# A four-layer graph network kernel: a short last piece of columns summed inside the piece in front of it, its lists placed between the next layer's prologue steps, and x loaded once

## The chip, the cores and the metric

The kernel runs on one NeuronCore of a Trainium2 chip. Five engines work side by side, each through its own instruction stream in order: TensorE (matrix products and transposes, called PE in the profile, with its weight loads as PEld), VectorE (DVE), ScalarE (ACT), GpSimd (POOL) and SyncE (SP), which issues nearly all DMAs here. The metric is the device time of one execution in microseconds; the time quoted is the median of three runs.

## The reference

Inputs are x, 2708 rows of 128 numbers, and adj, a sparse 2708 x 2708 matrix (about 0.6% of the off-diagonal entries are not zero, and the diagonal is full). Four layers follow one another; each normalises x, applies relu and adds its result to x.

```python
# layer 0
h = relu(layernorm(x))
x = x + (adj.T @ h) * (1 / adj.sum(axis=0))[:, None]      # infinite factors count as 0
# layer 1
h = relu(layernorm(x))
messages = gelu(s[:, None, :] + d[None, :, :] + msg_b)    # s, d: two products of h
aggregated = einsum('ijd,ij->id', messages, adj)
x = x + layernorm(gelu([h, aggregated] @ upd_w.T + upd_b) + h) * ln_w + ln_b
# layer 2: adj @ h and a GRU cell; layer 3: masked attention over adj, two heads
```

## The kernel before

**Tiling.** N = 2708 is cut into 22 row tiles of 128 (the last has 20 rows). GROUPS (line 48) puts them together in fours: six groups, five of 512 rows and a last one of 148. Layer 0 walks over pieces of columns c, one for each group, and inside a piece over the six row groups s. An item (c, s) is one block of adj, about 512 rows by 512 columns. LAST = 5 is the short piece, whose columns are the last 148 outputs and some 80 columns more for the lists.

**What an item does.** load_cut (line 299) brings the block of adj from HBM into one of RING = 4 buffers named a; the short piece's blocks z0 to z5 have buffers of their own. mask_near (line 317) copies, on GpSimd, the blocks of 124 columns that cross the diagonal and clears the diagonal in them, from the pool "marked" (6 buffers). list_cut (line 337) finds for each row and each block of 124 columns the eight greatest entries and their places on VectorE (max and max_index); layer 1 works from these lists. work_cut (line 353) transposes the block on TensorE, four 128 x 128 transposes into one of two PSUM banks p_T, copies it on ScalarE into one of seven buffers aT and lets SP write it to adjT in HBM for layers 2 and 3 (lines 382 to 387). Between the transposes stand the products of layer 0: adj.T @ h0, where h0 carries a column of ones that gives the degrees (line 368); the sums stay in PSUM over all six items of a piece, in the pool sump (line 287): two buffers of two banks. Then ScalarE counts entries by their sign (line 398), and on the diagonal items c = s it takes the diagonal out of a product that GpSimd made in the tile dg (lines 411 and 412, four buffers).

**What a finished piece needs.** invert (line 416) takes the reciprocal of the degrees, spread (line 435) scales the sums on ScalarE and adds them to x on GpSimd; sum_rows, sum_squares and normal_rows (lines 249 to 271) normalise the new rows on ScalarE and GpSimd, turn_rows (line 214) transposes them, destinations and split_destinations (lines 223 and 240) make the vectors d of layer 1 as three bf16 parts. enter and rows (lines 443 and 455) are the same steps on VectorE for pieces 4 and 5.

**The order.** All of this stands under manual_schedule: the order of the statements is the order on every engine, written out by hand. The loop over items (lines 473 to 529) is, for each item: mask_near, the lists, work_cut, load_cut of the item three ahead, then one step for an earlier piece. While piece 0 runs, ScalarE computes the row statistics of x that give h0. After the loop stand enter(4), the six items of the short piece without their lists, with turn_rows and destinations of piece 3 among them, and the masks of the short piece. The prologue of layer 1 (lines 993 to 1005) then names its steps one by one: list_last(s) makes the short piece's lists of one row group, rank, select_rows, describe, finish_rows, fetch_both and place prepare a row tile, pass_on and columns send its column numbers through HBM. After it come the periods of layer 1, one for each row tile, and layers 2 and 3.

**x.** Lines 78 and 79 clear the last tile of x and load its first four tiles; lines 460 and 461 do the same once more under the manual schedule, ahead of the first adj block. load_rest (line 80) brings the other tiles in six DMAs.

Of the kernel before, what the change touches and what calls it, by code (L numbers as in the profile page):

```python
# [30 lines left out]
P = 128  # L31
# [29 lines left out]
def listed_layers(ctx: ExitStack, tc: tile.TileContext, x, adj, w, out, flag):  # L61
# [18 lines left out]
    def load_rest():  # L80
        for t, k in GROUPS[1:-1]:
            nc.sync.dma_start(xs[:, t : t + k, :], x[t * P : (t + k) * P, :].rearrange("(t p) d -> p t d", p=P))
        nc.sync.dma_start(xs[:, FULL - 1, :], x[(FULL - 1) * P : FULL * P, :])
        nc.sync.dma_start(xs[0:TAIL, FULL, :], x[FULL * P : N, :])
# [98 lines left out]
    some4 = keep.tile([P, 4, NB, S], BF16, name="some4")  # L183
# [101 lines left out]
    marked = l0.enter_context(tc.tile_pool(name="l0n", bufs=6))  # L285
    turned = l0.enter_context(tc.tile_pool(name="l0t", bufs=7))
    sump = l0.enter_context(tc.tile_pool(name="l0p", bufs=2, space=PSUM))
# [65 lines left out]
    def work_cut(c, s):  # L353
# [6 lines left out]
        if s == 0:  # L360
            accs[c] = sump.tile([P, 2 * CH], F32, name="sums")
        pv = accs[c].rearrange("p (b x) -> p b x", b=2)[:, :, 0 : 2 * (D + 1)].rearrange("p b (q d) -> p b q d", q=2)

        def products(n):
            m = size(n)
            for q in range(tk):
                k, e = size(t0 + q), (t0 + q) * P - lo
                nc.tensor.matmul(  # L368
                    pv[0:k, q // 2, q % 2, :], a[0:m, n - g0, e : e + k], h0[0:m, n, :],
# [36 lines left out]
        if c == s:  # L406
            for q in range(gk):
                m = size(g0 + q)
                e = (g0 + q) * P - lo
                dg = marked.tile([P, P], F32, name="dg", bufs=4)  # L410
# [5 lines left out]
    def invert(g):  # L416
# [3 lines left out]
        if k == 4:  # L420
            sums = accs[g].rearrange("p (b x) -> p b x", b=2)[:, :, 0 : 2 * (D + 1)]
            sums = sums.rearrange("p b (q d) -> p b q d", q=2)[:, :, :, D]
            nc.vector.reciprocal(r.rearrange("p (b q) -> p b q", b=2), sums)
        else:
            nc.vector.reciprocal(r, last_sums[:, 0:k, D])
# [3 lines left out]
    def sums_of(g, q):  # L429

        if g == LAST:
            return last_sums[:, q, 0:D]
        return accs[g][:, q // 2 * CH + q % 2 * (D + 1) : q // 2 * CH + q % 2 * (D + 1) + D]
# [26 lines left out]
    nc.vector.memset(xs[:, NT - 1, :], 0.0)  # L460
    nc.sync.dma_start(xs[:, 0:4, :], x[0 : 4 * P, :].rearrange("(t p) d -> p t d", p=P))
# [11 lines left out]
    order = [(c, s) for c in range(LAST) for s in range(len(GROUPS))]  # L473
    for i, (c, s) in enumerate(order):
        g0, gk = GROUPS[s]
        mask_near(c, s)
# [7 lines left out]
        work_cut(c, s)  # L484
        if i > 0 and i - 1 + RING < len(order):
            load_cut(*order[i - 1 + RING])
        if c == LAST - 1:
            load_cut(LAST, s)

        if c == 0:  # L490
            for stage, g in (
                ((sum_rows, 1), (sum_rows, 2), (sum_squares, 1), (sum_rows, 3), (sum_squares, 2), (normal_rows, 1)),
# [7 lines left out]
        elif s == 0:  # L500
            invert(c - 1)
        elif s == 2:
            spread(c - 1)
        elif s == 3:
            sum_rows(*GROUPS[c - 1])
        elif s == 4:
            sum_squares(*GROUPS[c - 1])
        elif s == 5:
            normal_rows(h, *GROUPS[c - 1])
        if c > 1 and s == 0:  # L510
            turn_rows(c - 2)
        if c > 1 and s == 1:
            destinations(c - 2)
        if c > 1 and s == 3:
            split_destinations(c - 2)

# [15 lines left out]
    for s in range(len(GROUPS)):  # L532
        work_cut(LAST, s)
        if s == 1:
            turn_rows(LAST - 2)
        if s == 3:
            destinations(LAST - 2)
    for q, k in ((0, P), (1, TAIL)):
        nc.scalar.copy(last_sums[0:k, q, :], accs[LAST][0:k, q * (D + 1) : (q + 1) * (D + 1)])
# [27 lines left out]
    with (  # L567
# [411 lines left out]
        def list_last(s):  # L979
            g0, gk = GROUPS[s]  # L980
            for n in range(g0, g0 + gk):
                list_cut(LAST, s, n)

        def count_first(_):
            nc.vector.tensor_scalar(some4, val[:, 0:4, :, :], 0.0, None, ALU.is_gt)
            with nc.allow_low_precision("counts up to 8"):
                nc.vector.reduce_sum(rows_n[:, 0:4, :], some4, AX.X)
# [890 lines left out]
```

## Time and profile before

| | us |
|---|---|
| median of three runs | 1073.86 |
| the three runs | 1072.23, 1073.86, 1077.45 |
| the profiled execution | 1074.57 |
| its span, first to last instruction | 1072.8 |
| layer 0 and layer 1's prologue | 0 to 288 |
| layer 1's periods | 288 to about 590 |
| layers 2 and 3 | about 590 to the end |

The span in four stretches, with the busy time of each engine, the number of its instructions in brackets, then the TensorE clock that was granted (1.00 is full speed), the share of time that the 16 DMA engines were busy, and GB/s:

```profile
0.00:288.00 288.00, 212.64 (x1633) 190.45 (x1634) 226.75 (x1381) 194.29 (x505) 85.39 (x234) 0.88 0.70 235
288.00:590.00 302.00, 285.65 (x4089) 280.29 (x4087) 233.50 (x563) 193.06 (x593) 246.80 (x246) 0.98 0.33 104
590.00:790.00 200.00, 183.29 (x818) 103.13 (x816) 111.07 (x324) 69.00 (x186) 82.26 (x60) 0.96 0.48 159
790.00:1072.80 282.80, 248.77 (x2104) 240.07 (x2102) 222.53 (x476) 60.28 (x143) 57.69 (x59) 0.96 0.04 11
```

A line of a time-ordered view reads: start, duration, engine, line of the program, operation, output and input, shape, how many were merged into the line; in square brackets how long the engine stood idle before it and what released it.

### The profile page before, as it was taken

The page shows a single profiled execution, that of the slowest core. Times are in us where ns is not written, and L with a number is a line of the kernel's source. Part 1 is how long each engine was busy: PE and PEld are TensorE (multiplying, and loading weights), DVE is VectorE, ACT ScalarE, POOL GpSimd, SP SyncE. Part 2 cuts the span into 40 slices and gives each one's busy share as a digit, 9 for nine tenths or more (in the row PEclk, how much of TensorE's full clock was granted, in tenths as well). Part 3 has the DMA queues.
Part 4 walks back from the last instruction along what each step waited for, and adds up shares of the span by engine and source line. Part 5 has one row for each costly group of instructions (what it writes and reads, how often), then busy time and mean ns, then how long its engine had stood idle before and what let it go on. Part 6 is the DMA issues. An engine that isn't in the chain of part 4 may idle for free. (4 is left out here: it accounts for less than half of the span.)

```text
span 1072.8 us, 23407 instructions
## 1 busy us (share of the span) xinstructions
PE 930.4 (87%) x8632; PEld 813.9 (76%) x8632; DVE 793.9 (74%) x2742; ACT 516.6 (48%) x1427; POOL 472.1 (44%) x596
## 2 busy tenths in 40 slices
PE   3798887893599999999979968999979999999982
PEld 3798887862599999999879934444478899989981
DVE  7689979738877788878768164656678987997783
ACT  5978867763366567666736522433322200330142
POOL 5322312322598778897858263444320200250042
PEclk9899998985699999999989988999999999999996
DMA  8599898922143333332132046566410000000000
GB/s 258 193 341 317 272 362 269 322 78 80 55 125 124 116 105 123 115 99 93 57 109 83 29 168 214 187 221 227 123 38 21 7 9 1 2 15 6 2 16 15
DMA packets 77667, 133.91 MB, mean 125 GB/s; under 512 B 14044, under 2 KB 30032, under 8 KB 77542
## 3 DMA queue, kind: packets, MB, share of 16 engines
q1 hardware_dynamic: 75726, 129.52, 36.6%
q10 hardware_dynamic: 1816, 2.80, 0.9%
q8 instruction: 70, 1.15, 0.5%
q14 instruction: 55, 0.45, 0.1%
HBM read 85.67 MB, written 30.87 MB: 109 GB/s over the span
## 5 line engine op out<-in xcount | busy, mean ns | idle before, releaser
L725 POOL TENSOR_SCALAR put<-count,line,value 128x128 f32<-128x128 f32 x176 | 197.4, 1135 | 44.3 <-DVE value L714 31.2
L1124 PE MATMUL att<-hv,wt 128*128 128x129 f32 x1672 | 193.4, 276 | 9.0 <-DVE wt L1094 9.0
L1124 PEld LDWEIGHTS att<-hv,wt 128*128 128x128 f32 x1672 | 189.8, 192 | 11.9 <-DVE wt L1094 8.9
L807 PE MATMUL p_m<-s,sel 128*128 128x128 bf16 x1452 | 163.5, 222 | 8.0 <-ACT g L819 7.9
L811 PE MATMUL p_m<-d,cols 124*128 124x128 bf16 (+1 forms) x1452 | 164.2, 222 | 7.0 <-DVE cols L756 6.9
L1094 DVE SCALAR_TENSOR_TENSOR wt<-row,lift,mask 128x1024 f32<-128x1024 f32 (+1 forms) x132 | 138.7, 1082 | 23.2 <-PE att L1124 23.2
L121 POOL TENSOR_TENSOR n_r<-n_r,minus_half 128x4 f32<-128x4 f32 (+1 forms) x27 | 39.1, 1447 | 241.0 <-DVE n_r L120 237.3
L832 PE MATMUL agg<-put,g 128*128 128x128 f32 (+1 forms) x968 | 122.9, 279 | 0.0
L1263 PE MATMUL p_agg<-a,hs 128*128 128x512 f32 (+2 forms) x264 | 111.0, 563 | 12.5 <-DMA a<-adjT 12.5
L368 PE MATMUL sums<-h,a 128*128 128x129 f32 (+1 forms) x880 | 119.6, 284 | 0.0
L807 PEld LDWEIGHTS <-sel 128*128 128x128 bf16 x1452 | 105.0, 99 | 11.5 <-issue 10.9
L832 PEld LDWEIGHTS agg<-put,g 128*128 128x128 f32 x968 | 113.6, 192 | 0.0
L382 PE MATMUL p_T<-ident,a 128*128 128x128 f32 (+1 forms) x440 | 73.9, 291 | 44.1 <-ACT aT L386 32.8
L368 PEld LDWEIGHTS sums<-h,a 128*128 128x128 f32 (+1 forms) x880 | 111.3, 200 | 0.8
L811 PEld LDWEIGHTS <-cols 124*128 124x128 bf16 (+1 forms) x1452 | 104.2, 99 | 7.3 <-DVE cols L756 7.3
L734 ACT ACTIVATE put<-mine,value 128x128 f32<-128x128 bf16 x308 | 100.5, 391 | 0.0
L819 ACT ACTIVATE g<-p_m 128x512 f32<-128x512 f32 x132 | 72.6, 551 | 55.9 <-PE agg L832 43.5
L1263 PEld LDWEIGHTS p_agg<-a,hs 128*128 128x128 f32 (+1 forms) x264 | 48.2, 196 | 61.9 <-issue 53.5
L382 PEld LDWEIGHTS p_T<-ident,a 128*128 128x128 f32 (+1 forms) x440 | 54.6, 148 | 52.5 <-ACT aT L386 36.4
L349 DVE MAX8 val<-a 128x8 f32<-128x124 f32 x342 | 79.4, 274 | 19.0 <-DMA a<-in_adj 19.0
L351 DVE FIND_INDEX8 col<-val,a 128x8 uint16<-128x124 f32 x342 | 92.3, 283 | 0.0
L386 ACT COPY aT<-p_T 128x512 f32<-128x512 f32 (+2 forms) x122 | 66.1, 565 | 42.8 <-PE p_T L382 35.0
(284 smaller groups left out, 1560.1 us busy)
## 6 DMA issues: line engine op xcount, KB each, us to landing
adjT<-aT SPq DMA_DIRECT2D x105, 256.0 KB
a<-adjT SPq DMA_DIRECT2D x20, 1280.0 KB
spread<-passed SPq DMA_DIRECT2D x22, 704.0 KB
later<-sel SPq DMA_DIRECT2D x22, 616.0 KB
a<-in_adj SPq DMA_DIRECT2D x5, 1152.0 KB
a<-in_adj SPq DMA_DIRECT2D x5, 1120.0 KB
a<-in_adj SPq DMA_DIRECT2D x5, 1088.0 KB
a<-in_adj SPq DMA_DIRECT2D x5, 1056.0 KB
```

What stands on the lines that cost most here:

```text
L349: nc.vector.max(val[0:m, n, b, :], v)
L351: nc.vector.max_index(col[0:m, n, b, :], val[0:m, n, b, :], v)
L368: nc.tensor.matmul(pv[0:k, q // 2, q % 2, :], a[0:m, n - g0, e : e + k], h0[0:m, n, :], start=(n == 0 and q % 2 == 0), stop=(n == NT - 1), ...
L382: nc.tensor.transpose(p[0:k, i * iw + q * P : i * iw + q * P + m], a[0:m, q, e : e + k], ident[0:m, 0:m])
L725: nc.gpsimd.tensor_scalar(st["put", 0][:, b, :], count, st["line"][:, b : b + 1], st["value"][:, b : b + 1], ALU.is_equal, ALU.mult,)
L734: nc.scalar.activation(st["put", 1][:, b - HP, :], st["mine"][:, b - HP, :], AF.Identity, scale=st["value"][:, b : b + 1])
L807: nc.tensor.matmul(p[:, b - b0, :], st["sel"][:, b, :], s3[:, q, t % 2, :], start=(q == 0), stop=False)
L811: nc.tensor.matmul(p[:, b - b0, :], st["cols"][0:kb, b, :], d3[0:kb, b, q, :], start=False, stop=(q == 2))
L832: nc.tensor.matmul(agg, g[:, b - 4 * k, :], put, start=(b == 0), stop=False)
L1094: nc.vector.scalar_tensor_tensor(wt[:, 0:n], row[:, k, c : c + n], lift[:, j, k : k + 1], mask[:, j, c : c + n], op0=ALU.max, op1=ALU.mult,)
L1124: nc.tensor.matmul(banks[s // 3][:, s % 3, :], wt[:, q * P : (q + 1) * P], hv[:, j, k, :], start=(v < 2 and s // 3 not in touched), stop=( ...
L1263: nc.tensor.matmul(pa[:, 0:n], h[0:k, j, :], a[0:k, j - j0, 0:n], start=(j == 0), stop=(j == NT - 1))
```

## The change

x is loaded once: the second clearing and load are gone, and load_rest has three DMAs. The sums of a piece lie in one-bank tiles, four buffers of one bank instead of two of two, so that the short piece takes one. In the loop, mask_near is called one item ahead; load_cut and the invert of the piece before stand in front of work_cut; the short piece's blocks are loaded in piece 3 instead of piece 4; the steps for an earlier piece move one item forward or so; and from item (4,1) on each item of piece 4 is followed by work_cut of the short piece for the row group in front. Only the last row group of the short piece is left after the loop. Lists of the short piece are made row by row between the prologue's steps: row 0 before the first rank, rows 1 to 3 and their count behind it, the others later. The buffers of "marked" go from 6 to 8, those of dg from 4 to 2.

```diff
--- before.py
+++ after.py
@@ -78,9 +78,8 @@
     nc.vector.memset(xs[:, NT - 1, :], 0.0)
     nc.sync.dma_start(xs[:, 0:4, :], x[0 : 4 * P, :].rearrange("(t p) d -> p t d", p=P))
     def load_rest():
-        for t, k in GROUPS[1:-1]:
+        for t, k in ((4, 8), (12, FULL - 12)):
             nc.sync.dma_start(xs[:, t : t + k, :], x[t * P : (t + k) * P, :].rearrange("(t p) d -> p t d", p=P))
-        nc.sync.dma_start(xs[:, FULL - 1, :], x[(FULL - 1) * P : FULL * P, :])
         nc.sync.dma_start(xs[0:TAIL, FULL, :], x[FULL * P : N, :])
 
     ident = const.tile([P, P], F32, name="ident")
@@ -180,7 +179,7 @@
     ends4 = keep.tile([P, NB, R], BF16, name="ends4")
     rows_n = keep.tile([P, NT, NB], BF16, name="rows_n")
     ends = keep.tile([P, NT, NB], BF16, name="ends")
-    some4 = keep.tile([P, 4, NB, S], BF16, name="some4")
+    some4 = keep.tile([P, 3, NB, S], BF16, name="some4")
     later = keep.tile([P, NB, E], BF16, name="later")
     nc.gpsimd.memset(later, 0.0)
     xb = [keep.tile([P, NB, C], BF16, name=f"xb{q}") for q in range(2)]
@@ -282,9 +281,9 @@
     rows_a = l0.enter_context(tc.tile_pool(name="l0", bufs=RING))
     once0 = l0.enter_context(tc.tile_pool(name="l0h", bufs=1))
     pool = l0.enter_context(tc.tile_pool(name="l0k", bufs=2))
-    marked = l0.enter_context(tc.tile_pool(name="l0n", bufs=6))
+    marked = l0.enter_context(tc.tile_pool(name="l0n", bufs=8))
     turned = l0.enter_context(tc.tile_pool(name="l0t", bufs=7))
-    sump = l0.enter_context(tc.tile_pool(name="l0p", bufs=2, space=PSUM))
+    sump = l0.enter_context(tc.tile_pool(name="l0p", bufs=4, space=PSUM))
     turnp = l0.enter_context(tc.tile_pool(name="l0q", bufs=2, space=PSUM))
     h0 = once0.tile([P, NT, D + 1], F32, name="h0")
     offdiag = once0.tile([P, P], F32, name="offdiag")
@@ -358,15 +357,17 @@
         lo = window(c)[0]
         a = cuts[c, s]
         if s == 0:
-            accs[c] = sump.tile([P, 2 * CH], F32, name="sums")
-        pv = accs[c].rearrange("p (b x) -> p b x", b=2)[:, :, 0 : 2 * (D + 1)].rearrange("p b (q d) -> p b q d", q=2)
+            accs[c] = [
+                sump.tile([P, CH], F32, name="sums")[:, 0 : 2 * (D + 1)].rearrange("p (q d) -> p q d", q=2)
+                for _ in range(0, tk, 2)
+            ]
 
         def products(n):
             m = size(n)
             for q in range(tk):
                 k, e = size(t0 + q), (t0 + q) * P - lo
                 nc.tensor.matmul(
-                    pv[0:k, q // 2, q % 2, :], a[0:m, n - g0, e : e + k], h0[0:m, n, :],
+                    accs[c][q // 2][0:k, q % 2, :], a[0:m, n - g0, e : e + k], h0[0:m, n, :],
                     start=(n == 0 and q % 2 == 0), stop=(n == NT - 1), skip_group_check=True,
                 )
 
@@ -407,7 +408,7 @@
             for q in range(gk):
                 m = size(g0 + q)
                 e = (g0 + q) * P - lo
-                dg = marked.tile([P, P], F32, name="dg", bufs=4)
+                dg = marked.tile([P, P], F32, name="dg", bufs=2)
                 nc.gpsimd.tensor_tensor(dg[0:m, 0:m], a[0:m, q, e : e + m], ident[0:m, 0:m], ALU.mult)
                 nc.scalar.activation(
                     dg[0:m, 0:m], dg[0:m, 0:m], AF.Copy, accum_out=own[0:m, g0 + q : g0 + q + 1]
@@ -417,20 +418,15 @@
 
         t, k = GROUPS[g]
         r = inv[:, t : t + k]
-        if k == 4:
-            sums = accs[g].rearrange("p (b x) -> p b x", b=2)[:, :, 0 : 2 * (D + 1)]
-            sums = sums.rearrange("p b (q d) -> p b q d", q=2)[:, :, :, D]
-            nc.vector.reciprocal(r.rearrange("p (b q) -> p b q", b=2), sums)
-        else:
-            nc.vector.reciprocal(r, last_sums[:, 0:k, D])
+        for b in range(0, k, 2):
+            sums = last_sums if g == LAST else accs[g][b // 2]
+            nc.vector.reciprocal(r[:, b : b + 2], sums[:, :, D])
         nc.vector.tensor_scalar(lim[:, 0:k], r, FMAX, None, ALU.min)
         nc.vector.scalar_tensor_tensor(r, r, FMAX, lim[:, 0:k], op0=ALU.is_le, op1=ALU.mult)
 
     def sums_of(g, q):
 
-        if g == LAST:
-            return last_sums[:, q, 0:D]
-        return accs[g][:, q // 2 * CH + q % 2 * (D + 1) : q // 2 * CH + q % 2 * (D + 1) + D]
+        return (last_sums if g == LAST else accs[g][q // 2])[:, q % 2, 0:D]
 
     def spread(g):
 
@@ -457,8 +453,6 @@
         scale_rows(tiles_of(h, t, k), tiles_of(xs, t, k), *factors(*state.pop(("m", g))), AF.Relu)
 
     ordered.enter_context(tc.manual_schedule())
-    nc.vector.memset(xs[:, NT - 1, :], 0.0)
-    nc.sync.dma_start(xs[:, 0:4, :], x[0 : 4 * P, :].rearrange("(t p) d -> p t d", p=P))
     load_cut(0, 0)
     load_rest()
     for s in range(1, RING):
@@ -471,9 +465,9 @@
         nc.gpsimd.memset(wheres[q], 0.0)
 
     order = [(c, s) for c in range(LAST) for s in range(len(GROUPS))]
+    mask_near(0, 0)
     for i, (c, s) in enumerate(order):
         g0, gk = GROUPS[s]
-        mask_near(c, s)
         list_cut(c, s, g0)
         if i == 0:
             scale_rows(
@@ -481,15 +475,21 @@
             )
         for n in range(g0 + 1, g0 + gk):
             list_cut(c, s, n)
-        work_cut(c, s)
+        if c > 0 and s == 0:
+            invert(c - 1)
+        if i + 1 < len(order):
+            mask_near(*order[i + 1])
         if i > 0 and i - 1 + RING < len(order):
             load_cut(*order[i - 1 + RING])
-        if c == LAST - 1:
+        if c == LAST - 2:
             load_cut(LAST, s)
+        if i == 0:
+            sum_rows(*GROUPS[1])
+        work_cut(c, s)
 
         if c == 0:
             for stage, g in (
-                ((sum_rows, 1), (sum_rows, 2), (sum_squares, 1), (sum_rows, 3), (sum_squares, 2), (normal_rows, 1)),
+                ((sum_rows, 2), (sum_squares, 1), (sum_rows, 3), (sum_squares, 2), (normal_rows, 1)),
                 ((sum_rows, 4), (sum_squares, 3), (normal_rows, 2)),
                 ((sum_rows, 5), (sum_squares, 4), (normal_rows, 3)),
                 ((sum_squares, 5), (normal_rows, 4)),
@@ -497,22 +497,22 @@
                 (),
             )[s]:
                 stage(h0, *GROUPS[g]) if stage is normal_rows else stage(*GROUPS[g])
-        elif s == 0:
-            invert(c - 1)
+        elif s == 1:
+            spread(c - 1)
         elif s == 2:
-            spread(c - 1)
+            sum_rows(*GROUPS[c - 1])
         elif s == 3:
-            sum_rows(*GROUPS[c - 1])
+            sum_squares(*GROUPS[c - 1])
         elif s == 4:
-            sum_squares(*GROUPS[c - 1])
+            normal_rows(h, *GROUPS[c - 1])
         elif s == 5:
-            normal_rows(h, *GROUPS[c - 1])
+            turn_rows(c - 1)
         if c > 1 and s == 0:
-            turn_rows(c - 2)
-        if c > 1 and s == 1:
             destinations(c - 2)
-        if c > 1 and s == 3:
+        if c > 1 and s == 2:
             split_destinations(c - 2)
+        if c == LAST - 1 and s > 0:
+            work_cut(LAST, s - 1)
 
         if (c, s) == (0, 3):
             nc.sync.dma_start(msg_wT, w["msg_wT"])
@@ -529,14 +529,10 @@
             nc.gpsimd.tensor_tensor(src_self[:, 1, :], msg_wT[:, 0, :], msg_wT[:, 1, :], ALU.add)
 
     enter(LAST - 1)
-    for s in range(len(GROUPS)):
-        work_cut(LAST, s)
-        if s == 1:
-            turn_rows(LAST - 2)
-        if s == 3:
-            destinations(LAST - 2)
+    destinations(LAST - 2)
+    work_cut(LAST, LAST)
     for q, k in ((0, P), (1, TAIL)):
-        nc.scalar.copy(last_sums[0:k, q, :], accs[LAST][0:k, q * (D + 1) : (q + 1) * (D + 1)])
+        nc.scalar.copy(last_sums[0:k, q, :], accs[LAST][0][0:k, q, :])
     for s in range(len(GROUPS)):
         mask_near(LAST, s)
     l0.close()
@@ -976,27 +972,27 @@
             for k in range(1, GB):
                 put_more(t, k)
 
-        def list_last(s):
-            g0, gk = GROUPS[s]
-            for n in range(g0, g0 + gk):
-                list_cut(LAST, s, n)
-
-        def count_first(_):
-            nc.vector.tensor_scalar(some4, val[:, 0:4, :, :], 0.0, None, ALU.is_gt)
+        def list_last(n):
+            list_cut(LAST, n // 4, n)
+
+        def count_next(_):
+            nc.vector.tensor_scalar(some4, val[:, 1:4, :, :], 0.0, None, ALU.is_gt)
             with nc.allow_low_precision("counts up to 8"):
-                nc.vector.reduce_sum(rows_n[:, 0:4, :], some4, AX.X)
+                nc.vector.reduce_sum(rows_n[:, 1:4, :], some4, AX.X)
 
         def close_lists(_):
             ending.close()
 
         puts = ExitStack()
         for step, n in (
-            (list_last, 0), (count_first, 0), (rank, 0), (rows, 4), (select_rows, 0), (describe, 0), (turn_rows, 4),
-            (list_last, 1), (finish_rows, 0), (fetch_both, 0), (split_destinations, 3), (enter, 5), (rank, 1),
-            (destinations, 4), (select_rows, 1), (place, 0), (pass_on, 0), (sources, 0), (split_destinations, 4),
-            (rows, 5), (describe, 1), (list_last, 2), (turn_rows, 5), (destinations, 5), (finish_rows, 1),
-            (fetch_both, 1), (columns, 0), (split_destinations, 5), (place, 1), (rank, 2), (select_rows, 2),
-            (list_last, 3), (describe, 2), (list_last, 4), (list_last, 5), (close_lists, 0),
+            (list_last, 0), (count_rows, 0), (rank, 0), (list_last, 1), (select_rows, 0), (describe, 0), (rows, 4),
+            (list_last, 2), (list_last, 3), (count_next, 0), (turn_rows, 4), (split_destinations, 3),
+            (finish_rows, 0), (fetch_both, 0), (rank, 1), (destinations, 4), (enter, 5), (place, 0), (pass_on, 0),
+            (sources, 0), (select_rows, 1), (split_destinations, 4), (rows, 5), (describe, 1),
+            *((list_last, n) for n in range(4, 10)), (columns, 0), (turn_rows, 5), (destinations, 5),
+            (finish_rows, 1), (fetch_both, 1), (rank, 2), (split_destinations, 5), (place, 1), (select_rows, 2),
+            *((list_last, n) for n in range(10, 16)), (describe, 2), *((list_last, n) for n in range(16, NT)),
+            (close_lists, 0),
         ):
             step(n)
         putpool = puts.enter_context(tc.tile_pool(name="l1q", bufs=2, reuse_waits="tile"))
```

## The prediction

> **What bounds the kernel now.** I read the page first. TensorE is busy for 87% of the span, but the slices differ: the TensorE clock falls to 5 and 6 tenths near the tenth slice, and the DMA row is full only in the first quarter.
>
> ```profile
> span 1072.8 us, 23407 instructions
> PE 930.4 (87%) x8632; PEld 813.9 (76%) x8632; DVE 793.9 (74%) x2742; ACT 516.6 (48%) x1427; POOL 472.1 (44%) x596
> PEclk9899998985699999999989988999999999999996
> DMA  8599898922143333332132046566410000000000
> ```
>
> The change touches only what lies ahead of layer 1's period 0, so I cut the first 288 us by stage, at TensorE's first product of each piece: pieces 0 to 4, the short piece 5, layer 1's prologue. Columns: length; busy time of TensorE, weight loads, VectorE, ScalarE and GpSimd; clock; DMA share; GB/s.
>
> ```profile
> 0.00:62.60 62.60, 37.92 (x264) 34.74 (x264) 43.95 (x291) 45.29 (x139) 25.17 (x83) 0.92 0.72 234
> 62.60:95.80 33.20, 31.22 (x267) 29.70 (x265) 30.52 (x207) 25.78 (x61) 7.50 (x22) 1.00 0.98 336
> 95.80:132.80 37.00, 32.41 (x277) 30.96 (x276) 36.33 (x243) 30.06 (x72) 11.78 (x33) 1.00 0.92 297
> 132.80:176.70 43.90, 35.01 (x277) 33.33 (x276) 36.12 (x240) 31.56 (x75) 11.66 (x31) 0.92 0.89 308
> 176.70:215.60 38.90, 34.19 (x277) 32.63 (x276) 31.50 (x208) 29.31 (x70) 10.18 (x30) 0.96 0.94 315
> 215.60:240.80 25.20, 25.14 (x145) 15.90 (x145) 7.53 (x39) 14.87 (x42) 6.04 (x18) 0.86 0.26 83
> 240.80:288.00 47.20, 16.76 (x134) 13.18 (x134) 40.80 (x162) 17.42 (x54) 13.05 (x21) 0.57 0.18 62
> ```
>
> Each stage has its own limit. Piece 0 is ScalarE's serial stream (row statistics beside the copies). Pieces 1 to 4 are near balance between TensorE, VectorE and DMA. Piece 5 is TensorE alone. The prologue is VectorE's: of 40.05 us up to the third row tile's description it works 34.52. The order of time per engine shows the losses. First, VectorE stands still through piece 5:
>
> ```profile
> 241.02 0.18 DVE L648 CAST ends<-p_r 128x22 bf16<-128x22 f32 x1 [17.69 <-PE p_r L647]
> ```
>
> Second, in item (3,3) GpSimd's near masks sit behind an add that waits 10.90 us for ScalarE; the diagonal products follow the masks, ScalarE waits for those, and TensorE for ScalarE's copies:
>
> ```profile
> 157.32 1.27 POOL L441 TENSOR_TENSOR xs<-xs,part_x 128x512 f32<-128x512 f32 x1 [10.90 <-ACT part_x L440]
> 162.98 1.70 POOL L411 TENSOR_TENSOR dg<-a,ident 128x128 f32<-128x128 f32 x4
> 163.47 0.31 ACT L412 ACTIVATE dg<-dg 128x128 f32<-128x128 f32 x1 [1.14 <-POOL dg L411]
> 167.82 1.12 PE L382 MATMUL p_T<-ident,a 128*128 128x128 f32 x4 [4.51 <-ACT aT L386]
> ```
>
> Third, SP's first adj load waits behind x's second load, which waits for the first:
>
> ```profile
> SPq L461 <- DMA xs<-in_x: 2.5, 1, 2.5
> ```
>
> **What the Trainium skill says.** "TensorE: Matmul & The Clock Gate", Part 1: an idle window of about 3.4 us halves the clock until a busy window has passed. The trace agrees: after the 4.51 us gap the clock is 0.50 from 166 to 172 us. It is also 0.50 to 0.52 from 217 to 223 us, after a stretch with shorter gaps. The same page, "Architectural detail", calls ScalarE and VectorE strictly first in, first out, GpSimd so per core; the block above is such a chain. "DMA: Bandwidth & Descriptors", "Where 436 GB/s comes from", puts the HBM side at about 358 GB/s; stretches of 3 us here show 333 to 377, piece 1 holds 336.
>
> **The change, part by part.**
>
> *x once.* The second load of x's first four tiles (L461) and its memset go; the other six x loads become three. SP saves the 2.5 us wait and 0.4 us of issue. Row statistics began at 6.71 us when x landed the second time, ScalarE's first rows at 13.38. GpSimd's start memsets end at 6.27, 2.4 us before its pow at 8.69, so 2.4 us is what the chain can gain. Piece 0 is ScalarE's from there: -2.4. sum_rows(1) ahead of the first copies is the same work earlier.
>
> *Masks, loads and inverts earlier in the item.* mask_near of item i+1 now stands ahead of item i's diagonal products. It adds a wait for the next item's load, with the products and the x add behind it; the four-slot ring has that load issued three items earlier, so I take nothing. The 4.51 us gap goes, and with it four transposes and products at half clock (1.12+1.93+1.06+1.76 against 0.60+1.06 twice: 2.5). What is late next there is ScalarE itself: sign 2.1, diagonal 1.2, sum_squares 1.5, against the 3.4 us that two transpose banks hide, about 2 us of stall. -5 in piece 3. Elsewhere steps only trade places: normal_rows loses its wait (1.64 us gaps at 100 and 137), but spread(0) meets piece 1's diagonal products. Net 0. load_cut ahead of item i's four adjT writes makes SP wait for the last reader of item i-1, with those writes behind it. VectorE ends an item of piece 1 about 2.5 us after TensorE, the first write is ready about 1.3 us into the next, and seven copies are buffered: 0, at most 1 us an item.
>
> *dg buffers 4 to 2.* GpSimd cannot make all four products ahead. The third then waits for ScalarE's first pass: 0.30 + 0.46 + hand-over against 0.8, some 0.25 us; five diagonals, +1.0 (0 to 3). Splitting sums into one-bank tiles keeps the four banks; a second 0.17 us reciprocal lies beside TensorE.
>
> *z loads one piece earlier.* 2708 x 228 x 4 B = 2.47 MB move into piece 3. That stage moved 308 x 43.9 = 13.5 MB; of the 16.0 MB then, some 2.4 (loads for (4,1) and (4,2)) may land after its end, and 13.6 MB at 345 GB/s need 39.4 us. Piece 3 then takes about 39.9 us instead of 43.9 - 5 = 38.9: +1 (0 to 7.2, all of it uncovered).
>
> *The short piece inside piece 4.* One row group of it, warm:
>
> ```profile
> 226.54 0.60 PE L382 MATMUL p_T<-ident,z 128*128 128x128 f32 x4
> 226.97 0.71 PE L368 MATMUL sums<-h,z 128*128 128x129 f32 x4
> 227.62 0.60 PE L382 MATMUL p_T<-ident,z 128*20 128x128 f32 x4
> 228.06 2.21 PE L368 MATMUL sums<-h,z 128*128 128x129 f32 x12
> 230.20 0.66 PE L382 MATMUL p_T<-ident,z 128*128 128x128 f32 x4
> ```
>
> That is 3.66 us of TensorE. Piece 4 warm is 20 pairs of 1.33 (transpose and product start to start) = 26.7, its last group 3.95, turn_rows and destinations 1.3; with 5 x 3.66 = 18.3: 50.3. Behind each item ScalarE has sign 2.1 and a stage of 1.5, then two copies and a sign of the short piece, 2.0; TensorE's 3.66 us cover the first two. Uncovered: at (4,1) the first short products need the bank that spread(3) reads, 2.0; at (4,4) diagonal and normal_rows, 1.5; other gaps 0.5. Piece 4: 54.3. After it destinations(3) 0.9 and the last group 2.2: 57.4 until rank(0). Before: 38.9 + 25.2 = 64.1. -6.7 (-11 to 0).
>
> *Lists between the prologue's steps.* Before, the lists of rows 0 to 3 and their count lay in the 17.69 us hole. Now only row 0 must precede rank(0); rows 1 to 3 cost 3 x 0.89 = 2.7 on VectorE after it, counting three rows three quarters of 0.66 + 0.89, 1.2. Walking the new order with the old durations gives waits of 1.0 and 1.1 (ranks right behind fetches), 1.1 in sources, 1.3 for ScalarE before describe(1), about 5 in all against 5.5 now. +3.5 (0 to 5). What follows describe(2) keeps its order.
>
> Sum: -2.4 - 5 + 1 + 1 - 6.7 + 3.5 = -8.6. The profiled execution took 1074.57 us, 0.7 above the median of the three runs, 1073.86; from there, 1065.3.
>
> **The rivals.**
> - A (0.54), the sum: 1065.3, its own range 1059 to 1070.
> - B (0.18), the z loads bind. DMA is at 0.89 to 0.98 in pieces 1 to 4, which speaks for it; the prefetch and piece 4's light reads against. 7.2 us instead of 1: 1071.5, no change.
> - C (0.14), slower: SP is held. load_cut blocks the adjT writes until VectorE has finished item i-1; copies fill their seven buffers, ScalarE stops, then TensorE. For it: ScalarE already waits 3.4 us for writes in pieces 1 to 4, VectorE is full from 81 to 135 us. Against: a lag of only 2.5 us. At 1 us in each of the 18 items of pieces 1 to 3: 1083. It decides from 0.5 us an item (9 us), and makes the kernel slower by over 0.5% from 0.8.
> - D (0.14), more: no stall at (4,1) and (4,4), prefetch spares VectorE its lag, ranks don't wait. Another 6 us off: 1059.
>
> **How the numbers follow.** About 0.5%, 5.4 us, is what a measurement of this kernel can tell from no change. A (all but 0.02) and D, and 0.02 of B, are faster: 0.68; B's rest and the slip of A: 0.18; C: 0.14. The range 1058 to 1073 leaves out C and the ends of D.
>
> **What would show it.** In the changed profile: ScalarE's first rows near 11 us; no gap over 3 us in piece 3; short-piece products between those of piece 4; rank(0) near 229 us and no VectorE wait of 17 us ahead of it; the third row tile's v_r near 272 instead of 280.8; period 0 as before from there. Wrong if ScalarE waits for adjT writes by more than 10 us before 200, if piece 3 waits for loads, or if VectorE's prologue grows by more than 8 us.

## The result, and the profile after

The changed kernel takes 1077.89 us (median of 20 runs, 1072.57 to 1082.80) beside 1073.24 for the kernel before (20 runs). The ratio is 1.0042, with a 95% interval of 1.0027 to 1.0057: slower by 0.42%, some 4.5 us. The forecast was 1065.3, its range 1058 to 1073. The sign was wrong, and the time lies outside the range.

The lines of the page after that stand above for the kernel before:

```profile
span 1078.2 us, 23412 instructions
PE 934.4 (87%) x8632; PEld 816.0 (76%) x8632; DVE 795.4 (74%) x2748; ACT 516.6 (48%) x1427; POOL 471.0 (44%) x596
PEclk9899999985599999999989978999989999999996
DMA  8599899622133333333132045666410000000000
```

Busy times differ by at most 4 us and the slices look alike, so the page doesn't show where 4.5 us went. The stages of the kernel after, cut as before (length; busy time of TensorE, weight loads, VectorE, ScalarE and GpSimd; clock; DMA share; GB/s). Piece 5's products now lie inside piece 4, so the fifth line stands against two lines of before, and the last ends at the third row tile's v_r:

```profile
0.00:60.65 60.65, 37.82 (x265) 34.53 (x265) 45.02 (x295) 45.48 (x139) 25.04 (x83) 0.92 0.73 242
60.65:97.85 37.20, 32.66 (x266) 31.32 (x265) 34.77 (x232) 27.49 (x65) 9.88 (x29) 0.95 0.92 313
97.85:134.90 37.05, 32.46 (x277) 30.99 (x276) 35.13 (x233) 30.29 (x73) 11.21 (x31) 1.00 0.88 281
134.90:179.54 44.64, 34.55 (x277) 32.70 (x277) 35.43 (x233) 30.22 (x73) 11.00 (x30) 0.96 1.04 358
179.54:244.76 65.22, 60.16 (x422) 49.04 (x421) 33.35 (x212) 43.29 (x108) 14.62 (x41) 0.90 0.51 179
244.76:287.60 42.84, 14.04 (x120) 10.80 (x120) 37.29 (x148) 12.24 (x36) 8.26 (x12) 0.56 0.21 68
```

| stage, us | before | after | difference | forecast |
|---|---|---|---|---|
| piece 0 | 62.6 | 60.65 | -2.0 | -2.4 |
| piece 1 | 33.2 | 37.2 | +4.0 | 0, with all dg terms +1 |
| piece 2 | 37.0 | 37.05 | 0 | 0 |
| piece 3 | 43.9 | 44.6 | +0.7 | -4 |
| pieces 4 and 5, to rank(0) | 64.1 | 65.2 | +1.1 | -6.7 |
| rank(0) to the third v_r | 40.0 | 42.8 | +2.8 | +3.5 |

The sum, +6.8 ahead of layer 1's periods, is what has to be explained. The rest of the span is 1.4 us shorter in this execution, with the same program; all stage times here and below are of one execution each. The start and the prologue came out near the forecast; three stages did not.

*Piece 1.* ScalarE, GpSimd, SP and TensorE around the diagonal item of the kernel after, in order of time; in brackets the idle time ahead and what ended it (other lines between are left out):

```profile
68.42 4.58 SPq L388 DMA_DIRECT2D adjT<-aT  x4
...
72.07 0.59 ACT L387 COPY aT<-p_T 128x512 f32<-128x512 f32 x1 [2.11 <-DMA adjT<-aT]
72.55 1.91 ACT L399 ACTIVATE sign<-a 128x2048 bf16<-128x2048 f32 x1
...
74.92 0.86 POOL L412 TENSOR_TENSOR dg<-a,ident 128x128 f32<-128x128 f32 x2 [8.21 <-ACT dg L413]
75.81 0.74 SPq L314 DMA_DIRECT2D a<-in_adj  x2
...
76.13 1.12 ACT L436 ACTIVATE part_x<-sums,inv_deg 128x128 f32<-128x128 f32 x4
77.12 1.09 ACT L387 COPY aT<-p_T 128x512 f32<-128x512 f32 x2
77.75 3.66 SPq L388 DMA_DIRECT2D adjT<-aT  x4
77.78 0.66 PE L383 MATMUL p_T<-ident,a 128*128 128x128 f32 x4 [3.52 <-ACT aT L387]
```

With two dg buffers GpSimd makes the last two diagonal products only after ScalarE has read the first two: it stands for 8.21 us. These products read the block of adj, so its ring buffer isn't free, and SP's next load_cut, which needs that buffer, is issued only at 75.81. SP's own waits between 60 and 245 us of the kernel after show it (us in total, times, longest); neither row is there before:

```profile
SPq L308 <- POOL dg L412: 4.9, 2, 2.6
SPq L314 <- POOL dg L412: 2.7, 1, 2.7
```

The adjT writes stand behind this load, but the times don't show them held by it: the writes at 77.75 follow as soon as their first copies, begun at 77.12, are made, and ScalarE's wait of 2.11 us for an earlier write ends at 72.07, before SP's wait for dg begins at 73.1. That wait lies in a stretch in which the DMA engines are full (share 1.02 to 1.09 in each 3 us from 57 to 75 us). The fourth copy of the item is late by it, and sign, diagonal and spread in one go, 4.6 us, then leave TensorE 3.52 us without work. TensorE follows at half clock: its pair of transposes takes 1.06 and its products 1.92 at 79.38 to 82, against 0.60 and 1.06.

*Piece 3* is bound by DMA: share 1.04, 358 GB/s times 44.64 us = 16.0 MB. This is all the data that the stage and the moved loads ask for, and none was put off. The Trainium skill's "DMA: Bandwidth & Descriptors", "Where 436 GB/s comes from", has the same 358 for the HBM side. In these traces it is no ceiling: 405 GB/s were moved from 57 to 60 us of this kernel, and 391 from 78 to 81 us of the kernel before, where the forecast quoted 333 to 377. What shows that the stage is full is the share.

*Pieces 4 and 5.* TensorE in the kernel after, at its two waits:

```profile
195.01 1.35 PE L369 MATMUL sums<-h,z 128*128 128x129 f32 x4 [2.85 <-ACT part_x L436]
...
229.33 2.58 PE L383 MATMUL p_T<-ident,a 128*128 128x128 f32 x8 [1.78 <-ACT aT L387]
231.84 4.10 PE L369 MATMUL sums<-h,a 128*128 128x129 f32 x16
```

The first is the wait at (4,1) for the bank that spread(3) reads, forecast at 2.0; the second stands ahead of (4,5), where ScalarE had sign, four diagonal passes and normal_rows (1.6 us) in a row, forecast at 1.5. The sizes are near. What was not in the sum is what follows: eight transposes take 2.58 us and sixteen products 4.10, against 1.77 and 2.24 at full speed (the same instructions in the kernel with the stages moved, below). In steps of 3 us the clock reads 0.50 for 195 to 198, and 0.68, 0.50, 0.50, 0.61 from 228 to 240.

### The profile page after: what moved, and what is told of

The parts are those of the page before. It is cut to its first block, busy times and chain, and to the rows that moved or that the text cites. A ratio compares the mean times of both kernels' runs of the same rounds, so it can differ in the third digit from the quotient of the medians.

```text
span 1078.2 us, 23412 instructions
## 1 busy us (share of the span) xinstructions
PE 934.4 (87%) x8632; PEld 816.0 (76%) x8632; DVE 795.4 (74%) x2748; ACT 516.6 (48%) x1427; POOL 471.0 (44%) x596
## 5 line engine op out<-in xcount | busy, mean ns | idle before, releaser
L721 POOL TENSOR_SCALAR put<-count,line,value 128x128 f32<-128x128 f32 x176 | 198.5, 1138 | 44.6 <-DVE value L710 30.7
```

Source lines behind the costliest of these rows:

```text
L721: nc.gpsimd.tensor_scalar(st["put", 0][:, b, :], count, st["line"][:, b : b + 1], st["value"][:, b : b + 1], ALU.is_equal, ALU.mult,)
```

## The experiments

Each kernel was timed in five rounds beside the kernel before; the ratio is to that kernel, with its 95% interval. Differences between two variants below are differences of their ratios times 1073; with the intervals of both, each is uncertain by 2 to 4 us, so those of 4 us and less are to be read with care.

### What undoing one part of the change gives

Three parts undone one at a time, and a fourth kernel with the loads behind work_cut again. First the buffers of dg:

```diff
-                dg = marked.tile([P, P], F32, name="dg", bufs=2)
+                dg = marked.tile([P, P], F32, name="dg", bufs=4)
```

> The changed kernel with the dg buffers back at 4. Theory D (two dg buffers keep the last two diagonal products waiting for ScalarE, so SP, which waits for every reader of the slot before it issues the load three items ahead, stands still with the adjT writes behind it): SP's waits for dg (7.6 us in the changed kernel) go, ScalarE's waits for adjT writes fall from 13.7 us to about 10, piece 1 takes 34 to 35 us instead of 37.2, the kernel gains 2 to 4 us on the changed one. Rival (the z loads alone fill DMA): piece 1 stays at 37, under 1 us.

Measured: 1074.07, ratio 1.0005 (0.9989 to 1.0021), 4 us less than the change. Piece 1 went from 37.2 to 34.6 us, SP no longer waits for dg, and TensorE's gap in that item is 1.73 instead of 3.52:

```profile
75.00 0.66 PE L383 MATMUL p_T<-ident,a 128*128 128x128 f32 x4 [1.73 <-ACT aT L387]
```

ScalarE's sign, passes and spread are nearly as long in a row (4.1 us against 4.6), but the copies ahead of them come on time. What dg does is the same in every trace: ScalarE's four diagonal passes take 1.77 us in each of the five diagonal items of the four kernels with two buffers, and 1.26 or 1.27 in the six kernels after with four, because not only the third product comes late, by 0.27 us, but the fourth too. These 0.5 us reach TensorE, as its gap at item (2,2) of piece 2 shows, in the change and in this kernel:

```profile
121.80 0.66 PE L383 MATMUL p_T<-ident,a 128*128 128x128 f32 x4 [2.89 <-ACT aT L387]
117.99 0.66 PE L383 MATMUL p_T<-ident,a 128*128 128x128 f32 x4 [2.39 <-ACT aT L387]
```

In piece 1 the gap shrank by more than that, but not through dg. In the two kernels below that have the loads in piece 4 with four buffers, and the short piece behind the loop with two, the same gap reads:

```profile
76.44 0.66 PE L383 MATMUL p_T<-ident,a 128*128 128x128 f32 x4 [2.72 <-ACT aT L387]
76.95 1.11 PE L383 MATMUL p_T<-ident,a 128*128 128x128 f32 x4 [2.24 <-ACT aT L387]
```

In the first, with four buffers, the fourth copy waits 1.74 us for a write, as it did 2.11 in the change; in the second, with two, it doesn't wait. Without that wait two buffers add 0.5 us to the gap here too (2.24 against 1.73). Five items of 0.5 us make 2.5. In time, this pair gives 4 us, and the other pair that differs by dg alone, with the loads in piece 4, gives 1.2 (1.0010 with two buffers, the next run, and 0.9999 with four, below). Then the short piece's blocks, loaded in piece 4 as before:

```diff
-        if c == LAST - 2:
+        if c == LAST - 1:
             load_cut(LAST, s)
```

> The changed kernel with the short piece's blocks loaded in piece 4 again, each one item ahead of its use. Theory Z (piece 3 is bound by DMA in the changed kernel: 16 MB at 358 GB/s are its 44.6 us): piece 3 falls to 38 to 40 us, its ScalarE waits for adjT writes from 8.9 us to under 3, piece 4 with the short piece grows by 0 to 2 us; the kernel gains 3 to 5 us on the changed one. Rival (SP's order alone holds the writes): piece 3 stays over 43 us.

Measured: 1074.85, ratio 1.0010 (0.9996 to 1.0025), 3.4 us less than the change. Piece 3 fell from 44.6 to 41.9 us, not to the 38 to 40 expected, while the stretch from its end to rank(0), with both of its waits, took 66.4 against 65.2. The profiled execution, 1078.69, is 3.8 us above this kernel's median. The short piece behind the loop again, its loads in piece 3:

```diff
-        if c == LAST - 1 and s > 0:
-            work_cut(LAST, s - 1)
...
-    work_cut(LAST, LAST)
+    for s in range(len(GROUPS)):
+        work_cut(LAST, s)
```

> The changed kernel with the short piece's work back behind the loop; its loads stay in piece 3. Theory M (the merge is worth something, but its gain is eaten by the wait at (4,1) and by TensorE's half clock): from the end of piece 3 to rank(0) 62 to 66 us against 65.2 in the changed kernel, so within 2 us of it. If the merge by itself gains the 6.7 us that the prediction gave it, this kernel is 6 to 7 us slower than the changed one; if the merge is a loss it is 2 to 4 us faster.

Measured: 1077.33, ratio 1.0025 (1.0007 to 1.0043): 1.8 us less than the change, the intervals overlap. The forecast's largest gain, -6.7, is not there at all in this kernel. Last, the loads behind the work:

```diff
-        if i > 0 and i - 1 + RING < len(order):
-            load_cut(*order[i - 1 + RING])
-        if c == LAST - 2:
-            load_cut(LAST, s)
...
         work_cut(c, s)
+        if i > 0 and i - 1 + RING < len(order):
+            load_cut(*order[i - 1 + RING])
+        if c == LAST - 2:
+            load_cut(LAST, s)
```

> The changed kernel with load_cut (and the z loads) behind work_cut again, as before the change. Theory C (SP stands at the load until the slot's last reader is done, and the adjT writes behind it come late): ScalarE's waits for adjT writes fall from 13.7 us to 4 to 6, the kernel gains 3 to 5 us. Rival (DMA is full in any order): the waits stay above 10 us, the time within 1.5 us of the changed kernel.

Measured: 1077.16, ratio 1.0038 (1.0023 to 1.0053), as the change. ScalarE's waits for adjT writes went from 13.7 us to 0.5, and no time came of it: the waits went as theory C said, the time as its rival did. TensorE waits for a load instead, and piece 3 is as long as ever:

```profile
145.52 1.09 PE L383 MATMUL p_T<-ident,a 128*128 128x128 f32 x4 [5.06 <-DMA a<-in_adj]
```

```profile
133.70:178.20 44.50, 34.94 (x277) 33.30 (x278) 35.69 (x239) 30.40 (x73) 11.05 (x30) 0.92 1.00 341
```

In piece 3 the DMA engines are full in either order; the order only chooses who waits. Rival C's sign that was given for "wrong", over 10 us of ScalarE's waits for adjT, did appear, and is a symptom: the long waits lie in piece 3 (3.57 and 4.34 us), where DMA is full. With two dg buffers still there, putting load_cut behind the writes gained nothing, so this run doesn't support the chain from dg through SP's load to the writes either; the new wait for a load may hide a gain.

### The two steps that stand alone

The kernel before with one part of the change each, then with both: the second load of x away, and mask_near one item ahead.

```diff
     ordered.enter_context(tc.manual_schedule())
-    nc.vector.memset(xs[:, NT - 1, :], 0.0)
-    nc.sync.dma_start(xs[:, 0:4, :], x[0 : 4 * P, :].rearrange("(t p) d -> p t d", p=P))
```

> The kernel before with nothing changed but the second clearing and load of x's first tiles taken out. By the prediction's step: piece 0 ends 2.4 us earlier (60.3 instead of 62.7), the kernel gains 2 to 2.5 us, ratio 0.998. Rival: an earlier start is eaten by a later wait (pieces 1 to 3 wait for DMA or half clock): piece 0 ends earlier, the time moves by under 1 us.

Measured: 1070.52, ratio 0.9979 (0.9968 to 0.9990), 2.2 us. ScalarE's first rows start at 11.04 us instead of 13.38.

```diff
+    mask_near(0, 0)
     for i, (c, s) in enumerate(order):
         g0, gk = GROUPS[s]
-        mask_near(c, s)
...
+        if i + 1 < len(order):
+            mask_near(*order[i + 1])
         work_cut(c, s)
```

> The kernel before with mask_near called one item ahead and nothing else. By the prediction's step: the 4.51 us gap in item (3,3) and its half clock go, piece 3 falls from 43.9 to 38 to 40 us, the kernel gains 4 to 6 us. Rival: in this item ScalarE's own work and DMA come next, piece 3 keeps 42 us or more, the gain is under 2 us.

Measured: 1069.39, ratio 0.9962 (0.9944 to 0.9979), 4.1 us. In the kernel with masks ahead GpSimd's add no longer waits (10.90 us before), and TensorE's gap behind it is 2.38 instead of 4.51, the stall of "about 2" that the forecast left there:

```profile
159.47 1.27 POOL L441 TENSOR_TENSOR xs<-xs,part_x 128x512 f32<-128x512 f32 x1
```

```profile
167.52 1.07 PE L382 MATMUL p_T<-ident,a 128*128 128x128 f32 x4 [2.38 <-ACT aT L386]
```

So the expectation was right in size and wrong in place: only 1.2 us of the gain lie in piece 3 of its profile (42.7 against 43.9); 3.6 lie in pieces 4 and 5, where no stretch at half clock comes any more. Both parts together:

> The kernel before with x loaded once and mask_near one item ahead, nothing else of the change. Theory (these two steps hold and add up, 2.2 + 4 us alone): 1066 to 1068, ratio 0.993 to 0.995. Rival (they overlap, since both only move the same wait in piece 3): 1069 to 1070.

Measured: 1067.02, ratio 0.9935 (0.9912 to 0.9957), 7.0 us: they add up, against -7.4 in the forecast.

### The steps beside the short piece

If the two waits of piece 4 and the half clock behind them undo the gain, then moving the stages for piece 3 one item forward within piece 4 should bring it back: spread(3) then stands in (4,0), ahead of the first short products, and normal_rows in (4,3), not on the diagonal item. Once with four dg buffers, once with the loads in piece 4 besides:

```diff
-        elif s == 1:
+        elif s + (c == LAST - 1) == 1:
             spread(c - 1)
-        elif s == 2:
+        elif s + (c == LAST - 1) == 2:
             sum_rows(*GROUPS[c - 1])
...
```

> The changed kernel with four dg buffers and, in piece 4 alone, the steps for piece 3 one item earlier (spread in (4,0), sum_rows in (4,1) and so on), so that the short piece's first products find their bank free and item (4,4) has no normal_rows beside its diagonal. Theory G (each short gap of TensorE there is paid twice, by the gap and by some 9 us at half clock behind it): the gaps of 2.85 and 1.78 us go, the half clock from 225 to 240 us goes, from the end of piece 3 to rank(0) 57 to 59 us instead of 62.4 with four dg buffers alone, 4 to 5 us faster than that kernel. Rival (the half clock follows from the thin products of the short piece themselves): half clock stays near the end of piece 4, 62 us, under 1.5 us gained.

> The changed kernel with the three things that the theories call its costs undone at once: four dg buffers, the short piece's blocks loaded in piece 4, piece 3's steps one item earlier in piece 4. If they are the causes and add up: piece 1 near 34.6 us, piece 3 near 40, from its end to rank(0) 57 to 60, the kernel 8 to 12 us faster than the changed one and 4 to 7 us faster than the one before, ratio 0.993 to 0.997. If they overlap (the same DMA and clock limits come back elsewhere): no faster than with four dg buffers alone, ratio near 1.000.

Measured: 1065.00, ratio 0.9930 (0.9903 to 0.9957), and 1062.95, ratio 0.9898 (0.9874 to 0.9922). The stages are worth 8 us beside four dg buffers, more than the 4 to 5 expected, and the second ratio lies below the 0.993 to 0.997 given. And with the stages where the change put them, buffers and loads as before:

> The kernel after with four dg buffers and the short piece's blocks loaded in piece 4, its short piece still summed inside piece 4 with the steps where the change put them. Theory (three separate losses: two dg buffers, the loads in piece 3, the steps inside piece 4): only the third is left, the gaps at (4,1) and (4,5) are still there, and the time is 1070 to 1072, some 8 us above the same kernel with the steps one item earlier (1062.95). Rival (the steps did nothing once the buffers and loads are as before; the gain came from these): 1063 to 1065.

Measured: 1073.06, ratio 0.9999 (0.9984 to 1.0015): 1 us above the band given, no gain over before, and 10.8 us above the same kernel with the stages moved. The stretch from the end of piece 3 to rank(0), first of this kernel, then of the one with the stages moved:

```profile
174.24:240.54 66.30, 61.88 (x421) 50.80 (x421) 33.34 (x212) 43.01 (x108) 14.64 (x41) 0.87 0.63 208
```

```profile
173.03:228.26 55.23, 54.29 (x421) 45.19 (x420) 33.35 (x212) 42.49 (x108) 13.75 (x38) 1.00 0.75 249
```

The same 421 products: at clock 1.00 TensorE is busy for 54.29 of 55.23 us, at 0.87 for 61.88 of 66.30. Of the 11.1 us, 7.6 are TensorE's busy time at the lower clock and 3.5 its waits, mainly these two of the first kernel:

```profile
189.49 0.82 PE L369 MATMUL sums<-h,z 128*128 128x129 f32 x4 [2.71 <-ACT part_x L436]
224.95 2.42 PE L383 MATMUL p_T<-ident,a 128*128 128x128 f32 x8 [1.28 <-ACT aT L387]
```

With the stages moved no wait of TensorE over 1.2 us is left between piece 3 and rank(0).

### What the short piece and the lists are worth then

From the fastest kernel so far (1062.95), the short piece put behind the loop again, with the diff shown above:

> Four dg buffers, loads in piece 4, steps one item earlier in piece 4, and the short piece behind the loop again instead of inside piece 4. Theory (the step of -6.7 us for the short piece inside piece 4 was of the right size, and only the steps beside it took it away): piece 4 and the short piece up to the first rank take 61 to 63 us against 55.2, and the time is 1068 to 1071. Rival (the short piece inside piece 4 is worth nothing, as the pair of kernels with and without it showed before; the steps alone made the gain): 1062 to 1064.

Measured: 1067.08, ratio 0.9931 (0.9912 to 0.9951), just under the band given. Its stretch:

```profile
173.58:232.77 59.19, 54.79 (x421) 45.27 (x421) 33.35 (x212) 42.64 (x107) 14.54 (x41) 1.00 0.68 230
```

59.2 us against 55.2, where 61 to 63 was expected: the short piece inside piece 4 gives about 4 us by the stretches and 3.5 by the ratios, not 6.7, since without low clock its old place costs less than the 64.1 from which the forecast started. The intervals of the two ratios overlap a little. And from the same fastest kernel, the prologue's steps in the order of the kernel before, with the lists of rows 0 to 3 ahead of rank(0):

```diff
-            (list_last, 0), (count_rows, 0), (rank, 0), (list_last, 1), (select_rows, 0), (describe, 0), (rows, 4),
-            (list_last, 2), (list_last, 3), (count_next, 0), (turn_rows, 4), (split_destinations, 3),
...
+            *((list_last, n) for n in range(0, 4)), (count_rows, 0), (count_next, 0), (rank, 0), (rows, 4),
+            (select_rows, 0), (describe, 0), (turn_rows, 4), *((list_last, n) for n in range(4, 8)),
...
```

> Four dg buffers, loads in piece 4, steps one item earlier, short piece inside piece 4, but the prologue's steps and lists in the order of the kernel before, so that the lists of rows 0 to 3 stand ahead of the first rank. Theory (VectorE bounds the prologue, and with the 17 us hole gone these lists cost their own time wherever they stand, but hold up the first rank here): third v_r 2 to 4 us later than with the change's order, 1064 to 1067. Rival (VectorE has had its hole inside piece 4 and makes these lists there in any order): 1062 to 1064, no difference.

Measured: 1061.10, ratio 0.9882 (0.9862 to 0.9902), the lowest of all. The theory is excluded; the rival holds, or the old order is even 1.7 us better, which the intervals don't decide. Its prologue and VectorE's lists ahead of rank(0):

```profile
228.75:269.44 40.69, 13.84 (x119) 10.74 (x120) 35.10 (x128) 11.44 (x33) 6.69 (x12) 0.58 0.21 70
```

```profile
227.83 0.39 DVE L582 TENSOR_SCALAR some<-val 128x176 bf16<-128x176 f32 x1
...
229.07 0.70 DVE L981 TENSOR_REDUCE rows_n<-some 128x66 bf16<-128x528 bf16 x1
229.69 0.17 DVE L644 CAST ends<-p_r 128x22 bf16<-128x22 f32 x1
```

rank(0) starts at 228.75 instead of 228.26, and the prologue takes 40.7 us instead of 42.85. In the change's order VectorE stands still for 2.07 us ahead of rank(0) in that kernel, and makes rows 1 to 3 afterwards; here it makes them in that wait. The last piece still leaves VectorE a hole ahead of piece 4's reciprocal, of 13.13 us in both, and of 18.96 in the change. Counted from VectorE's first copy of rank(0) to the third v_r, the stretch is 42.6 us in all nine kernels with the change's order and 39.8 in all five with the old one, so the 2.8 us between them are no matter of one execution.

## Why the prediction was wrong

In ratios, the way from the kernel before to the change: x once and masks ahead 0.9935; the other edits but the short piece inside piece 4, with dg, loads and stages set right, 0.9931; with it inside, 0.9898; the stages put where the change has them, 0.9999; the two dg buffers and the loads in piece 3, 1.0042. So some 7 + 0.4 + 3.5 us are gained and 10.8 + 4.6 lost.

- *x once, -2.4*: right, 2.2 alone and 2.0 in the profile of the change.
- *Masks ahead, -5*: right in size alone, 4.1. The chain (add, masks, dg, ScalarE, TensorE) was read rightly from the profile. The place was only half right, since most of it shows as clock in pieces 4 and 5. In the change piece 3 was 0.7 us longer all the same, since its limit was another by then.
- *load_cut ahead of the work, 0*: right; putting it back changed nothing.
- *"dg buffers 4 to 2 ... +1.0 (0 to 3)"* was mis-sized: "some 0.25 us" an item is 0.51 in all four kernels with two buffers, since the fourth product waits as the third does (0.27 us), so five diagonals make 2.5 us. In time four buffers gave 4.0 us in one pair of kernels (1.0042 to 1.0005) and 1.2 in another (1.0010 to 0.9999). The forecast also looked at VectorE as the last reader of a block, while GpSimd now reads it until ScalarE is done, and SP's load waits up to 2.7 us for that; but no trace shows this wait to reach TensorE. *"Net 0"* for piece 1 failed by the late write and the half clock behind the gap as well; why the write was late in some kernels and not in others stays open.
- *"z loads one piece earlier ... +1 (0 to 7.2)"* was mis-sized, within its range: undoing it gave 3.4 us in two pairs of kernels and 0.6 in a third. The step that failed is "some 2.4 may land after its end": piece 3 moved 16.0 MB, not 13.6.
- *"The short piece inside piece 4 ... -6.7 (-11 to 0)"* failed, and turned the sign: with the steps where the change has them the stage grew by 1.1 us. Of its terms the two stalls were near (2.85 and 1.78 for 2.0 and 1.5). Left out was the clock after them: "no half clock" was implied by adding 50.3 us of warm work to 4.0 of stalls. TensorE was busy for 60.16 us in that stretch instead of 54.29. The warm sum itself was good: 57.4 was forecast, and 55.2 reached once the waits were gone. The forecast itself quoted half clock after 4.51 us, and again after shorter gaps in piece 5, so it had the reason to put a price on each stall.
- *Lists, +3.5*: right in size (2.8 in the profile), in part by luck: it was priced as the cost of filling the hole, and the hole remains, only earlier; with the old order 40.7 us are enough.
- *Rivals*: C gave the right sign and the wrong mechanism (18 small waits in pieces 1 to 3, 1083). B was in part true. None held the low clock behind the new waits, the largest single loss.

## What to carry to other kernels

When work is packed between TensorE's steps, price each wait that it adds twice: the wait, and the time at half clock that may follow it; then move the steps that make the wait, not the packed work. The same merge gained nothing with spread and normal_rows one item later and about 4 us with them one item earlier. Fewer buffers between two engines also hold what the first of them reads: here two dg buffers held an adj block, and the block held SP's load for up to 2.7 us. Before such a chain is called the cause, its times have to be put in order: here the late write came before it.

## What the runs showed of the hardware

The length of a wait did not by itself decide whether the clock fell. A wait of 1.78 us at (4,5) was followed by some 10 us at half clock in the change, and one of 1.28 us at the same place by as much with four dg buffers and the loads in piece 4; while 2.89 us at 121.80 in the change, within piece 2, left the clock at 1.00. The traces show two things that go with it.

*Where the wait falls.* In each of the 14 traces the clock changes only at whole steps of 3.41 us from its other changes; in the change at 164.25, 167.67, 194.97, 198.39, 229.11 and 239.35, which are 1, 8, 1, 9 and 3 steps apart. Nearly the same wait in piece 2, 2.39 us with four dg buffers and the stages moved, 2.38 with the loads in piece 4 besides, cost the first kernel a step at half clock and the second nothing. In the first it lies within one step (first line; the clock of the step behind it is in the second), in the other it is split over two (third and fourth line):

```profile
115.04:118.45 3.41, 1.02 (x10) 0.83 (x9) 3.41 (x25) 3.15 (x15) 1.39 (x2) 1.00 0.95 315
118.45:121.87 3.42, 3.42 (x19) 3.42 (x17) 3.42 (x25) 1.71 (x3) 0.00 (x0) 0.50 0.79 276
114.35:117.76 3.41, 1.88 (x17) 1.69 (x16) 3.41 (x25) 3.41 (x19) 0.10 (x1) 1.00 0.82 253
117.76:121.17 3.41, 2.56 (x23) 2.56 (x24) 3.41 (x24) 2.40 (x6) 1.29 (x2) 1.00 1.04 391
```

*What TensorE works on.* The step of the change in piece 2 that kept the clock, and the one in piece 4 after which it fell:

```profile
119.88:123.29 3.41, 1.50 (x13) 1.50 (x14) 3.41 (x25) 2.93 (x10) 1.39 (x2) 1.00 0.90 273
225.69:229.11 3.42, 1.86 (x11) 0.91 (x10) 0.00 (x0) 3.14 (x13) 0.86 (x2) 1.00 0.00 0
```

TensorE is busy for longer in the second, but with the short piece's products, six of its eleven only 20 columns wide. From 15 to 250 us in the 14 traces the clock fell after all 37 steps at full clock in which products and transposes of full 128 x 128 blocks filled up to 0.41 of the step, and after none of the 452 in which they filled 0.45 or more; after steps with blocks of 20 rows or columns among them it fell at shares up to 0.78. That narrow work alone doesn't do it: with the stages moved it is all there, at clock 1.00.

These are readings of traces; no run varied the place of a wait or the width of the products alone, and what brings the clock back, after one step at 164.25 and after three at 229.11, stays open. The Trainium skill ("TensorE: Matmul & The Clock Gate", Part 1) names an idle window of about 3.4 us. The length agrees with the step, but no step had to be idle: even the 3.52 us of piece 1 lie across two, the second of them (75.51 to 78.92) busy for a third.
